# A group's maxima made into rows: one transposition and four masked copies in place of four transpositions and one copy

## The chip, the cores and the metric

The kernel runs on one core of a Trainium2 chip. The metric is the time of one execution on the device, in microseconds (us). The engines are named as the profile names them: PE is TensorE (matrix products), PEld its loads of stationary operands, DVE is VectorE, ACT is ScalarE, POOL is GpSimd, SP is the engine that issues most transfers. Each engine works through its own instructions in order and waits on semaphores for the others.

## The reference

A transformer block over x of shape (4, 512, 512): layer norm, attention over a context of 512 rows of width 256, residual, layer norm, and a feed-forward layer with ternary weights, residual. The attention has 32 heads of width 16:

```python
q = (x @ Wq).reshape(b, n, 32, 16)
k, v = jnp.split(ctx @ Wkv, 2, axis=-1)        # each to (b, 512, 32, 16)
q = apply_axial_rope(q, pos_map); k = apply_axial_rope(k, ctx_pos_map)
logits = jnp.einsum("bqhd,bkhd->bhqk", q, k) / 4
w = jax.nn.softmax(logits, axis=-1)
attn = jnp.einsum("bhqk,bkhd->bqhd", w, v).reshape(b, n, 512)
x = x + attn @ Wout + bout
...
h = gelu(bitlinear(layernorm(x), w_fc)); x = x + bitlinear(h, w_proj)
```

The change concerns the softmax alone: for each query and head the maximum over the keys is taken away from the logits before the exponential.

## The kernel before

**Groups and units.** The 32 heads of 4 batches are worked on in 32 groups `i` of four heads (`HG`), eight groups to a batch. A group has eight units `u`; each unit covers two heads. There are two passes over a group.

The first pass, `logits` (L423) and `maxima` (L437), has queries on the partitions: two products make a 128x1024 tile `lp` in PSUM (two heads, 512 keys each), and one DVE reduction takes the negated maximum along the keys, so that a group's eight units leave `mx`, 128 queries by 4 tiles of queries by 4 heads. At the last unit of the group `maxima` splits these 16 columns into a rounded high part (L441) and the rest (L442) and puts both into `mparts`, a tile of which two stand ready (groups take turns), filled with zeros once at the start (L168).

The second pass, `exponentials` (L462, L470, L474), has keys on the partitions: two products make `sp`, the transposed logits, and two more add the maxima to it. For these the maxima have to be rows: `mrows` has the queries along its free side (512 of them), and `sel` holds ones in the rows that belong to the wanted head. ACT then takes the exponential of the 128x1024 tile into `es`. `weigh` (L484) multiplies `es` with the values, eight products for every two units, into `av`.

**The maxima as rows.** `place_maxima` makes `mrows`. In `mparts` each of the four tiles of queries has a 128-column block of its own, in which 4 columns of each half are filled. Four transpositions on the PE (L449), one for each tile of queries, put the rows into one PSUM bank `mtp` of 128x512, and one ACT copy with a cast (L453) brings the bank to SBUF.

**What sets the order.** All five engines run in an order that the program writes out (`manual_schedule`). The units of the second pass (`s`) and those of the first pass (`l`, 13 to 15 units ahead) form one stream, cut in bursts of three. After each burst come the products of `weigh` that are due, and then at most one chore that finishes: a chore is a piece of other PE work with one PSUM bank `ps_t` of its own (a single buffer), such as the projections of queries, keys, values (`heads`, `values`: `qpq`, `kpk`, `vp`), the transpositions of normalised x (`tokens`: `xtp`) and the output projection (`projected`: `op`). What a chore leaves to other engines is put off to the next bursts (`put_off`): for `place_maxima`, the ACT copy at the head of the next burst. Chores are paid for with a credit that grows by 1.3 with each burst (1.1 late); `place_maxima` is urgent and goes in any case, but its cost, the last number of its `Chore`, is taken from the credit that other chores then lack. `lp` and `sp` share a pool of three PSUM tiles (`ps_s`), so a product into a fourth waits for the DVE reduction or the ACT exponential that reads the first.

**Elsewhere.** `make_sel` (L173) makes `sel` once before the first group. Rotations of queries and keys (`swap`, L353 to L359) run on DVE and POOL. The weights of the feed-forward layer are read in 32 chunks during the attention, summed (L569) and turned into signs by POOL (`low`, L585) and DVE (`ws`, L583). After the attention, from about 580 us, the feed-forward stage runs with almost nothing but L928 and L966 on the PE.

Of the kernel before, what the change touches and what calls it, by code (L numbers as in the profile page):

```python
# [9 lines left out]
F32 = mybir.dt.float32  # L10
F32R = mybir.dt.float32r
AF = mybir.ActivationFunctionType
ALU = mybir.AluOpType
AX = mybir.AxisListType

P = 128
# [15 lines left out]
def xattn_ffn(  # L32
# [13 lines left out]
    nc = tc.nc  # L46
# [3 lines left out]
    NT = S // P  # L50
# [17 lines left out]
    const = ctx.enter_context(tc.tile_pool(name="const", bufs=1))  # L68
# [25 lines left out]
    apool = attn.enter_context(tc.tile_pool(name="apool", bufs=2))  # L94
# [51 lines left out]
    ident = const.tile([P, P], F32, name="ident")  # L146
# [17 lines left out]

    mparts = []
    for i in range(2):
        mp = apool.tile([P, NT, P], F32, name=f"mparts{i}", tag=f"mparts{i}", bufs=1)
        nc.gpsimd.memset(mp, 0.0)  # L168
        mparts.append(mp)
    sel_col = const.tile([P, 2], F32, name="sel_col")  # L170
    sel = const.tile([P, 2, P], F32R, name="sel")

    def make_sel():  # L173
        nc.vector.tensor_reduce(
            sel_col,
            ident.rearrange("p (h c) -> p h c", h=2)[:, :, 0:4].rearrange(
                "p h (l r) -> p r h l", r=2
            ),
            AX.XY,
            ALU.add,  # L180
        )
        for r in range(2):
            nc.vector.tensor_scalar(sel[:, r, :], ones, sel_col[:, r : r + 1], None, ALU.mult)

# [54 lines left out]
    def put_off(k, f, end=0):  # L239
        later[end].setdefault(k, []).append(f)  # L240
# [174 lines left out]
    mx = {}  # L415
    mrows = {}
# [15 lines left out]
    def maxima(i, u, lp):  # L432

        t, r = divmod(u, 2)
        if u == 0:
            mx[i] = small.tile([P, NT, 2, 2], F32, name=f"mx{i}", tag="mx")
        nc.vector.tensor_reduce(mx[i][:, t, :, r], lp, AX.X, ALU.max, negate=True)  # L437
        if u == NU - 1:
            mp = mparts[i % 2].rearrange("p t (h c) -> p t h c", h=2)
            high = mp[:, :, :, 0:2]  # L440
            nc.vector.tensor_copy(high.bitcast(F32R), mx[i])  # L441
            nc.vector.tensor_tensor(  # L442
                mp[:, :, :, 2:4].bitcast(F32R), mx[i], high, ALU.subtract
            )

    def place_maxima(i):
        def step(tp, _):
            for t in range(NT):
                nc.tensor.transpose(tp[:, t * P : (t + 1) * P], mparts[i % 2][:, t, :], ident)  # L449

        def post(tp, k):
            mrows[i] = apool.tile([P, S], F32R, name=f"mrows{i}", tag="mrows")
            put_off(k + 1, lambda: nc.scalar.copy(mrows[i], tp))  # L453

        return Chore(f"mtp{i}", 1, step, post, 0.7)

    def exponentials(i, u):

# [248 lines left out]
    for what in "kq":  # L707
        chore(heads(0, 1, what))
    make_sel()
    load_x(1)  # L710
    nc.sync.dma_start(bout_sb, bout.to_broadcast([P, D]))
# [3 lines left out]
    for n in range(FIRST + 1):  # L715
        k0 += 1
        run(k0)
        if n < FIRST:
            lps[n] = logits(*divmod(n, NU))
        if n > 0:  # L720
            maxima(*divmod(n - 1, NU), lps.pop(n - 1))
        run(k0, 1)
        if fill:
            if fill[0].go():
                fill[0].post(fill[0].p, k0)
                fill.pop(0)
        if n == NU + 1:
            c = place_maxima(0)
            c.go()
            c.post(c.p, k0)  # L730
# [56 lines left out]
    for k, burst in enumerate(bursts):  # L787
        run(k)
        for kind, s in burst:
            i, u = divmod(s, NU)  # L790
            if kind == "l":
                lp = logits(i, u)
                maxima(i, u, lp)
                if u == NU - 1:
                    urgent.append((k + 1, place_maxima(i)))
                continue
# [16 lines left out]
            if u in (2, 6):  # L813
                c = 2 * i + u // 4
# [26 lines left out]
        while due and due[0][0] <= k:  # L841
            _, j, c, e = due.pop(0)
# [17 lines left out]
        while True:  # L860
            if open_chore is None:
# [5 lines left out]
                elif queue and queue[0].ready <= k and not used_bank and credit >= queue[0].cost:  # L867
                    c = queue[0]
# [51 lines left out]
    def xbank(name):  # L920
        return ps_x.tile([P, KD, P], F32, name=name, tag="x")
# [96 lines left out]
    with tc.manual_schedule(engines=ordered):  # L1018
# [15 lines left out]
        for n in range(len(steps) + 4):  # L1034
            on = n < len(steps)
            if on:
                b, f = steps[n]
# [5 lines left out]
            if on and b == 0 and 6 <= f < 6 + NT:  # L1043
                t = f - 6
                p = xbank(f"op{B - 1}_{t}").rearrange("p k n -> p (k n)")
# [8 lines left out]
                i = (B - 1) * NT + t  # L1054
                nc.vector.tensor_tensor(x_sb[:, i, :], p, x_sb[:, i, :], ALU.add)
            if on and b + 1 < B:
                at = (10, 11, 13, 14) if b == 0 else (6, 9, 12, 14)
                for t in range(NT):
                    i = (b + 1) * NT + t
# [95 lines left out]
```

## Time and profile before

| | us |
|---|---|
| median of 3 runs | 858.34 |
| lowest, highest | 857.26, 858.89 |
| the profiled execution, its own time | 856.57 |
| its span, first to last instruction | 854.8 |
| PE busy, DVE busy, ACT busy, POOL busy | 812.2, 619.7, 456.7, 287.1 |
| from 60 to 560 us (attention) | PE idle 11.1 of 500 |
| the four transpositions of L449, one group: their start to the next product | 0.58 to 0.59 |
| the copy of L453 | 0.587, 32 times |
| the exponential of L474 | 1.025, 256 times |
| the reduction of L437 | 1.216 mean, 256 times |

The profile is one execution, taken by the hardware. A busy share counts the time in which an instruction of that engine is under way; products on the PE overlap, so what a product really takes is read from the distance between starts, not from its own duration. An idle time is given with what ended it: the last of the things that the instruction waited for. The chain is the work that ended last, followed back from the end.

### The profile page before, as it was taken

The page shows a single profiled execution, that of the slowest core. Times are in us where ns is not written, and L with a number is a line of the kernel's source. Part 1 is how long each engine was busy: PE and PEld are TensorE (multiplying, and loading weights), DVE is VectorE, ACT ScalarE, POOL GpSimd, SP SyncE. Part 2 cuts the span into 40 slices and gives each one's busy share as a digit, 9 for nine tenths or more (in the row PEclk, how much of TensorE's full clock was granted, in tenths as well). Part 3 has the DMA queues.
Part 4 walks back from the last instruction along what each step waited for, and adds up shares of the span by engine and source line. Part 5 has one row for each costly group of instructions (what it writes and reads, how often), then busy time and mean ns, then how long its engine had stood idle before and what let it go on. Part 6 is the DMA issues. An engine that isn't in the chain of part 4 may idle for free.

```text
span 854.8 us, 13868 instructions
## 1 busy us (share of the span) xinstructions
PE 812.2 (95%) x5364; PEld 428.3 (50%) x5364; DVE 619.7 (72%) x852; ACT 456.7 (53%) x603; POOL 287.1 (34%) x287
## 2 busy tenths in 40 slices
PE   4699999999999899999999999998999999999996
PEld 1134433344333333433333334336668888888885
DVE  4789778788878988878678877825455864864755
ACT  2146766665665545666555665576234544554442
POOL 3017274653833564586515731301000100100000
PEclk9799999999999999999999999999999999999999
DMA  6875777567586576967645657432000100100101
GB/s 205 303 286 194 259 259 228 186 217 262 191 301 200 167 252 220 308 211 264 208 149 183 221 205 272 158 119 98 1 1 1 49 1 1 50 0 1 50 1 49
DMA packets 75561, 135.25 MB, mean 158 GB/s; under 512 B 10728, under 2 KB 12648, under 8 KB 74984
## 3 DMA queue, kind: packets, MB, share of 16 engines
q1 hardware_dynamic: 75088, 133.72, 45.8%
q8 instruction: 42, 0.69, 0.3%
q10 hardware_dynamic: 408, 0.66, 0.2%
q14 instruction: 23, 0.19, 0.1%
HBM read 79.30 MB, written 55.05 MB: 157 GB/s over the span
## 4 chain that ended last, share of the span: by engine, by line
PE 78%; DVE 12%; DMA 6%; issue 1%; ACT 1%; SPq 1%; POOL 1%; ACTq 0%; DVEq 0%; POOLq 0%
PE hp L928 14%; PE fp L966 14%; PE av L484 12%; PE sp L462 7%; PE lp L423 7%; DVE mx L437 7%; PE sp L470 5%; PE qpq L285 4%; PE op L285 4%; PE vp L285 3%; PE kpk L285 3%; PE op L1047 2%; PE mtp L449 1%; DVE ws L583 1%; DMA c_sb<-in_ctxT 1%
## 5 line engine op out<-in xcount | busy, mean ns | idle before, releaser
L437 DVE TENSOR_REDUCE mx<-lp 128x2 f32<-128x1024 f32 x256 | 305.3, 1216 | 86.0 <-PE lp L423 85.6
L474 ACT ACTIVATE es<-sp 128x1024 f32<-128x1024 f32 x256 | 254.5, 1025 | 146.6 <-PE sp L470 138.3
L484 PE MATMUL av<-es,va 128*32 128x512 f32 x1024 | 136.0, 604 | 0.0
L462 PE MATMUL sp<-q_st,k_st 64*128 64x512 f32 x512 | 115.1, 446 | 8.9 <-DVE mx L437 7.7
L423 PE MATMUL lp<-k_st,q_st 64*128 64x512 f32 x512 | 113.0, 437 | 9.4 <-DMA q_st<-q_d 7.4
L936 ACT ACTIVATE h<-hp,gam_fc 128x512 f32<-128x512 f32 x64 | 44.0, 688 | 129.1 <-PE hp L928 129.1
L966 PE MATMUL fp<-wproj,hh 128*128 128x512 f32 x256 | 103.5, 404 | 0.0
L928 PE MATMUL hp<-dTh,wfc 128*128 128x512 f32 x256 | 100.4, 392 | 1.2 <-ACT dTh L657 1.2
L470 PE MATMUL sp<-mrows,sel 64*128 64x512 f32 x512 | 101.2, 390 | 0.2 <-ACT mrows L453 0.2
L966 PE MATMUL fp<-wproj,hl 128*128 128x512 f32 x256 | 101.1, 395 | 0.0
L928 PE MATMUL hp<-dTl,wfc 128*128 128x512 f32 x256 | 100.4, 392 | 0.2 <-DVE dTl L658 0.2
L955 DVE TENSOR_TENSOR acc<-acc,h 128x512 f32<-128x512 f32 x56 | 38.7, 691 | 73.5 <-ACT h L936 73.5
L462 PEld LDWEIGHTS sp<-q_st,k_st 64*128 64x128 f32 x512 | 48.0, 184 | 83.1 <-DVE mx L437 42.6
L423 PEld LDWEIGHTS lp<-k_st,q_st 64*128 64x128 f32 x512 | 48.3, 185 | 80.8 <-ACT es L474 40.3
L523 POOL TENSOR_TENSOR aT<-aT,rb 128x512 f32<-128x512 f32 x16 | 21.1, 1320 | 133.3 <-DMA rb<-rden_d 112.1
L285 PE MATMUL qpq<-xT,wq_sb 128*32 128x512 f32 x512 | 62.3, 594 | 0.8 <-ACT xT L321 0.7
L928 PEld LDWEIGHTS hp<-dTh,wfc 128*128 128x128 f32 x256 | 48.2, 188 | 12.6 <-ACT dTh L657 2.1
L966 PEld LDWEIGHTS fp<-wproj,hl 128*128 128x128 f32 x256 | 48.3, 189 | 11.3 <-issue 0.7
L966 PEld LDWEIGHTS fp<-wproj,hh 128*128 128x128 f32 x256 | 48.2, 188 | 11.2 <-issue 0.7
L928 PEld LDWEIGHTS hp<-dTl,wfc 128*128 128x128 f32 x256 | 48.1, 188 | 11.0 <-DVE dTl L658 0.5
L470 PEld LDWEIGHTS sp<-mrows,sel 64*128 64x128 f32 x512 | 48.5, 185 | 5.9 <-ACT mrows L453 0.9
L196 POOL TENSOR_SCALAR r_a<-mv 128x1 f32<-128x1 f32 x16 | 4.7, 292 | 130.3 <-DVE mv L633 130.3
(129 smaller groups left out, 1036.0 us busy)
## 6 DMA issues: line engine op xcount, KB each, us to landing
k_st<-k_d SPq DMA_DIRECT2D x32, 512.0 KB
q_st<-q_d SPq DMA_DIRECT2D x32, 512.0 KB
k_d<-sh_k SPq DMA_DIRECT2D x32, 256.0 KB
k_d<-sl_k SPq DMA_DIRECT2D x32, 256.0 KB
q_d<-sh_q SPq DMA_DIRECT2D x32, 256.0 KB
q_d<-sl_q SPq DMA_DIRECT2D x32, 256.0 KB
av_d<-avs SPq DMA_DIRECT2D x32, 256.0 KB
wm<-in_wfcT SPq DMA_DIRECT2D x16, 256.0 KB
```

Source lines behind the costliest of these rows:

```text
L285: nc.tensor.matmul(p[j * HP : (j + 1) * HP, :], w[:, j * HP : (j + 1) * HP], x, start=start, stop=stop,)
L423: nc.tensor.matmul(lp[:, h, :], q_st[i][rows, r, t * P : (t + 1) * P], k_st[i][rows, r, :], start=True, stop=True,)
L437: nc.vector.tensor_reduce(mx[i][:, t, :, r], lp, AX.X, ALU.max, negate=True)
L462: nc.tensor.matmul(sp[:, h, :], k_st[i][rows, r, c * P : (c + 1) * P], q_st[i][rows, r, :], start=True, stop=False,)
L470: nc.tensor.matmul(sp[:, h, :], sel[rows, r, :], mrows[i][rows, :], start=False, stop=True)
L474: nc.scalar.activation(es, sp, AF.Exp, scale=1.0 / math.sqrt(HD))
L484: nc.tensor.matmul(av[j * HP : (j + 1) * HP, :], va[b % 2][:, c, v0 : v0 + HP], es[r][:, h, :], start=c == 0, stop=c == NT - 1,)
L523: nc.gpsimd.tensor_tensor(aT[b][:, n, :], aT[b][:, n, :], rb, ALU.mult)
L928: nc.tensor.matmul(hp, wfc_sb[k][:, f * P : (f + 1) * P], dT[b][half][:, k, :], start=half == 0 and k == 0, stop=half == 1 and k == KD - 1,)
L936: nc.scalar.activation(hid[b, f], hp, AF.Gelu, scale=gam_fc[:, 0:1])
L955: nc.vector.tensor_tensor(acc[b][0], old, x, ALU.add)
L966: nc.tensor.matmul(outs[b][t], parts[b, f][half][:, t * P : (t + 1) * P], wproj_sb[f], start=half == 0 and f == 0, stop=half == 1 and f == ...
```

## The change

`mparts` shrinks from four blocks to one of 128 columns: each half of 64 columns now holds 16 filled ones, ordered by head of the pair, high or low part, and tile of queries. One transposition gives a 128x128 block whose rows are the maxima of one head, part and tile. ACT then writes it four times, once for each tile of queries, into the four quarters of `mrows`, each time multiplied by a column of a mask that is one in the rows of that tile and zero in the others. `sel` picks all eight rows of a head, of which six hold zeros for any one query. `make_sel` makes the mask with one more reduction. The cost of the chore falls from 0.7 to 0.3.

```diff
-        mp = apool.tile([P, NT, P], F32, name=f"mparts{i}", tag=f"mparts{i}", bufs=1)
+        mp = apool.tile([P, P], F32, name=f"mparts{i}", tag=f"mparts{i}", bufs=1)
         nc.gpsimd.memset(mp, 0.0)
...
+    mask = const.tile([P, NT], F32, name="mask")
     def make_sel():
-        nc.vector.tensor_reduce(
-            sel_col,
-            ident.rearrange("p (h c) -> p h c", h=2)[:, :, 0:4].rearrange(
-                "p h (l r) -> p r h l", r=2
-            ),
-            AX.XY,
-            ALU.add,
-        )
+        rows = ident.rearrange("p (h c) -> p h c", h=2)[:, :, 0 : 4 * NT]
+        for dst, view in (
+            (sel_col, rows.rearrange("p h (r c) -> p r h c", r=2)),
+            (mask, rows.rearrange("p h (c t) -> p t h c", t=NT)),
+        ):
+            nc.vector.tensor_reduce(dst, view, AX.XY, ALU.add)
...
         if u == NU - 1:
-            mp = mparts[i % 2].rearrange("p t (h c) -> p t h c", h=2)
-            high = mp[:, :, :, 0:2]
+            mp = mparts[i % 2].rearrange("p (h c) -> p h c", h=2)[:, :, 0 : 4 * NT]
+            high, low = (
+                mp.rearrange("p h (r l t) -> p l t h r", r=2, l=2)[:, n] for n in range(2)
+            )
             nc.vector.tensor_copy(high.bitcast(F32R), mx[i])
-            nc.vector.tensor_tensor(
-                mp[:, :, :, 2:4].bitcast(F32R), mx[i], high, ALU.subtract
-            )
+            nc.vector.tensor_tensor(low.bitcast(F32R), mx[i], high, ALU.subtract)

     def place_maxima(i):
         def step(tp, _):
-            for t in range(NT):
-                nc.tensor.transpose(tp[:, t * P : (t + 1) * P], mparts[i % 2][:, t, :], ident)
+            nc.tensor.transpose(tp[:, 0:P], mparts[i % 2], ident)

         def post(tp, k):
             mrows[i] = apool.tile([P, S], F32R, name=f"mrows{i}", tag="mrows")
-            put_off(k + 1, lambda: nc.scalar.copy(mrows[i], tp))
-
-        return Chore(f"mtp{i}", 1, step, post, 0.7)
+
+            def spread():
+                for t in range(NT):
+                    nc.scalar.mul(
+                        mrows[i][:, t * P : (t + 1) * P], tp[:, 0:P], mask[:, t : t + 1]
+                    )
+
+            put_off(k + 1, spread)
+
+        return Chore(f"mtp{i}", 1, step, post, 0.3)
```

## The prediction

> **What bounds the kernel now.** First the page's busy times and chain, then the shares by stretch, then the single place of the change in the timeline.
>
> ```profile
> PE 812.2 (95%) x5364; PEld 428.3 (50%) x5364; DVE 619.7 (72%) x852; ACT 456.7 (53%) x603; POOL 287.1 (34%) x287
> ...
> PE 78%; DVE 12%; DMA 6%; issue 1%; ACT 1%; SPq 1%; POOL 1%; ACTq 0%; DVEq 0%; POOLq 0%
> ```
>
> The PE is busy for 95% and holds 78% of the chain. The Trainium skill (Perfetto Trace Analysis, "Identifying the Most-Contended Engine") warns that matmul busy time is a poor measure, because products overlap. So I looked at starts: in the attention the same two products follow each other at the same distance again and again (0.23 us for a pair of L462, L470 or L423), so the PE really has no gaps there. By stretch (PE, PEld, DVE, ACT, POOL busy):
>
> ```profile
> 60.00:160.00 100.00, 99.99 (x790) 40.64 (x788) 80.40 (x106) 62.95 (x76) 57.20 (x52) 1.00 0.66 219
> 260.00:360.00 100.00, 94.36 (x726) 37.87 (x728) 86.83 (x110) 56.50 (x66) 51.09 (x41) 1.00 0.66 221
> ```
>
> The PE leads, DVE is second with 80 to 87%, ACT has over a third free on average. In the second stretch DVE takes over in places. PE work that goes is therefore worth most of its time, but not all of it.
>
> The change sits here; the first fence is L449 and its reader, the second the timeline around one group (start, duration, instruction, idle before):
>
> ```profile
> L449 PE MATMUL mtp<-ident,mparts x128: 272/273/330, 50.1 to 561.3; 128*128 128x128 f32 x128
> L453 ACT CAST mrows<-mtp x32: 578/587/595, 50.8 to 562.9; 128x512 fp32r<-128x512 f32 x32
> ```
>
> ```profile
> 164.45 1.94 ACT L474 ACTIVATE es<-sp 128x1024 f32<-128x1024 f32 x2
> 164.97 0.66 PE L449 MATMUL mtp<-ident,mparts 128*128 128x128 f32 x4
> 165.56 0.49 PE L423 MATMUL lp<-k_st,q_st 64*128 64x512 f32 x2
> 165.90 0.50 PE L462 MATMUL sp<-q_st,k_st 64*128 64x512 f32 x2
> 166.24 0.39 PE L470 MATMUL sp<-mrows,sel 64*128 64x512 f32 x2
> 166.27 0.59 ACT L453 CAST mrows<-mtp 128x512 fp32r<-128x512 f32 x1
> 166.46 0.47 PE L423 MATMUL lp<-k_st,q_st 64*128 64x512 f32 x2
> ```
>
> The four transpositions take 0.59 us from their start to the next product. The first alone shows as 0.33 and all four as 0.66, so three more add 0.33: 0.11 us each, though each has a duration of 273 ns. The skill gives about 275 ns for a transposition inside a kernel (TensorE: Matmul & The Clock Gate, "Part 4: PE-mode transpose"); the duration agrees, but the price on a full PE is the 0.11.
>
> **The change part by part, for 32 groups.**
>
> *Three transpositions less.* 0.33 us a group, at most 32 x 0.33 = 10.6 us. What of it counts depends on what ends next, and the order written out gives only three places:
> - Between `weigh` and a product `lp` (9 groups: 95.3, 146.0, 195.4, 244.6, 299.7, 351.7, 403.5, 453.7, 499.7 us). ACT is idle before the copy and again before the next exponential. Whole gain: -3.0 us.
> - Between `weigh` and a product `sp` (12 groups). Four end in a wait for DVE (181.1, 281.5, 386.2, 487.6; the products after them wait up to 1.66 us for L437) and one leads into a stretch that DVE holds (533.2): nothing. Three (129.7, 229.9, 336.0) have a chore behind the burst: -1.0. The rest below, with ACT.
> - Right behind a product `sp` (11 groups), as in the fence. There ACT has two exponentials to work off; the second ends at 164.45 + 1.94 = 166.39, and the `lp` at 166.46 needs its bank. The PE arriving 0.33 earlier would wait for it. Eight of the eleven are pinned like this to within 0.1 us (-0.05 each), three have 0.3 to 0.5 of room (113.5, 319.8, 421.6): -0.4 - 0.9 = -1.3.
>
> *One ACT copy becomes four scaled ones.* Nothing in the trace is 128x128 from PSUM with a scale that is a column, so I bound it. Nearest row: the gelu L936, 128x512 from PSUM with such a scale, 688 ns; less 384 elements at 0.833 is 368 ns. The skill (ScalarE: Activation LUTs, "What ACT_TABLE_LOAD costs") has 186 ns plus 0.833 an element plus 93 for a column operand, 386 ns here, and an overlap of 93 ns back to back; the trace agrees on the overlap (two exponentials of 1.025 in 1.94, 0.11 less than their sum). So a start every 0.27 to 0.28, and four take 3 x 0.275 + 0.37 = 1.19 us against 0.587. Ends: without overlap 1.47; with the overhead hidden as in a copy followed by an exponential (starts 0.46 apart for 512 elements, so about 0.04 over the elements) 0.15 a piece, 0.8. I take 1.19: ACT is held 0.6 us longer, 20 us in all, hidden by its idle third except where an exponential behind it frees a bank for the PE. In the first place the exponential came 0.96 after the copy began and can now come at 1.10: 0.14 late, covered by the chore that follows. In the second it came at 0.72 and is now 0.38 late; where no chore follows (82.5, 439.2) the two `lp` behind it lose some 0.2 of the 0.33: -0.13 each, -0.3. In the third, it is late by 0.6, but ACT then idled 1.7 us. Two groups have the copy itself on the path: the first (50.1; L470 waited 0.25 for L453) +0.3, and the last (560.9, where exponentials are the chain) +0.6. The bank of `ps_t` comes free at the earliest 0.3 us before the next chore wants it: nothing, up to 0.2 a group if the four take 1.47.
>
> *DVE.* The two writes into `mparts` keep 16 elements and get one more stride; median 232 and 177 ns. Their maxima, 1282 and 1210, are stalls: the skill says that DVE and POOL share a port pair under an exclusive lock (SBUF — State Buffer, "SBUF: two separate sides"), and the long ones have a POOL instruction under way. (L441 for 1.28 us at 210.31, under the POOL's L356 from 210.28 to 211.56). I take no change, 0; at one end the longer pattern may cost 0.02 a group, at the other it may escape the lock, which would free up to (460 - 175) + (346 - 175) ns of DVE a group by the means, worth something only in the DVE stretches: -1 us at most. The mask costs one reduction of 128x32, by the 152 ns of L174 some 0.18 us, between L174 and L183; the first L437 began at 35.24, right behind, and 0.2 is made up while DVE next waits 1.34 for the PE: 0. If not, +0.2.
>
> *POOL.* Two memsets of 532 ns become about 204 each (as those of 128x128 at the start): nobody waits for them.
>
> *The credit.* Each group leaves 0.4 more: chores come up to six units earlier from unit 88 on (the transpositions for batch 3 at unit 130 instead of 136, `vp2_2` at 91 instead of 94), and with them their rotations on DVE and POOL, the transfers of `k_d`, `q_d` on SP and the loads of the next context. The last ones before the end stay, because they are tied to later units; between units 204 and 214 the PE is less full in both orders. PE work in total is the same, so 0; but POOL does its `low` (L585) in other company, and DVE waits in order for it (3.9 us in three waits now): +-2 us.
>
> **Sum:** -3.0 - 1.0 - 1.3 - 0.3 + 0.9 = -4.7 us; 856.57 becomes 851.9. The profiled execution lies 1.8 under the median of the runs, so against the median I forecast 858.34 - 4.7 = 853.6.
>
> **Rivals.**
> - *Everything counts* (the pinned places move along, as the exponentials are themselves fed by the PE): -10.6, 847.7. For it: 20 of the 32 transpositions are in the chain. Against: the bank waits above.
> - *A wash*: ACT takes back all that the PE gives, 858. PEld waits 40.3 us in 70 places for L474 already.
> - *Slower*: ACT decides. Place: the first and second exponential behind the four copies, whose banks the next `lp` products take. Price: the 0.63 of longer hold less the 0.33 saved, +0.3 a group, as soon as there is no slack between the end of an exponential and the product that reuses its bank; in half of the groups 16 x 0.3 = +4.8, 863. It decides if the four take over 1.3 us, or if earlier chores make ACT fuller where the copies fall. Against: chores follow the burst in most groups.
> - *The change doesn't do it* (more waits in the transposition): the instruction stream shows one L449 and four ACT writes a group, so no.
>
> **Numbers.** Forecast 0.46 (849 to 857), everything 0.14, wash 0.16, slower 0.24. A measurement here tells apart about 0.2%, 1.7 us. Faster: forecast, all of the first rival and a little of the wash, 0.62; same 0.15; slower 0.23. The range takes in the first rival and most of the last, 847.5 to 862.
>
> **What would show it.** L449 with 32 instructions and 0.25 us from its start to the next product; ACT on `mrows` 128 instructions of about 370 ns, four in 1.2 us; more idle time of PEld before `lp` ended by L474 than 40.3 us; L437 still about 1.2 us. I am wrong if four copies take far from 1.2 us, or if the stalls of DVE behind `low` or L449's neighbours grow by more than 3 us.

## The result and the profile after

| | before | changed kernel |
|---|---|---|
| median of 5 runs, us | 858.34 | 866.26 |
| lowest, highest | 857.26, 861.04 | 862.59, 867.39 |
| ratio, with its 95% interval | | 1.0079 [1.0051, 1.0107] |
| profiled execution: span, mean granted clock | 854.8, 0.993 | 864.5, 0.983 |
| feed-forward stage, in the trace | 273.4 | 273.4 |

The kernel became slower by 0.8%, where 0.55% faster was forecast. The feed-forward stage takes the same 273.4 us in both traces (from 581.39 to 854.8 and from 591.09 to 864.5), so the whole loss lies in the attention. Line numbers have moved: L449 is now L447, L453 is L454, L437 is L436, L441 and L442 are L442 and L443, L462, L470, L474 and L484 are L467, L475, L479 and L489, L423 is L422, L285 is L284, L585 is L590.

First the instructions that were exchanged, each tile's list of the changed kernel (count, then shortest, median and longest duration in ns):

```profile
L447 PE MATMUL mtp<-ident,mparts x32: 300/328/329, 50.8 to 570.0; 128*128 128x128 f32 x32
L454 ACT ACTIVATE mrows<-mtp,mask x128: 358/370/399, 51.1 to 572.8; 128x128 fp32r<-128x128 f32 x128
L442 DVE CAST mparts<-mx x32: 182/205/1279, 50.2 to 567.6; 128x16 fp32r<-128x16 f32 x32
L443 DVE TENSOR_TENSOR mparts<-mx,mparts x32: 187/192/1231, 50.5 to 567.8; 128x16 fp32r<-128x16 f32 x32
```

One transposition instead of four, four ACT writes of 370 ns, DVE writes that are hardly different. By these lines the change cost nothing. The page shows where time went; first two of its lines before the change, then those after:

```profile
L437 DVE TENSOR_REDUCE mx<-lp 128x2 f32<-128x1024 f32 x256 | 305.3, 1216 | 86.0 <-PE lp L423 85.6
L462 PEld LDWEIGHTS sp<-q_st,k_st 64*128 64x128 f32 x512 | 48.0, 184 | 83.1 <-DVE mx L437 42.6
```

```profile
PE 809.3 (94%) x5268; PEld 421.2 (49%) x5268; DVE 616.0 (71%) x853; ACT 472.1 (55%) x699; POOL 286.8 (33%) x287
...
PE   4699999999999899989999899898999999999996
...
PEclk9799999999999999999999899899999999999998
...
L436 DVE TENSOR_REDUCE mx<-lp 128x2 f32<-128x1024 f32 x256 | 305.8, 1216 | 99.7 <-PE lp L422 99.4
...
L467 PEld LDWEIGHTS sp<-q_st,k_st 64*128 64x128 f32 x512 | 48.4, 186 | 90.1 <-DVE mx L436 54.0
```

The PE lost 96 instructions and is busy 2.9 us less, in a span that is 9.7 us longer: it stands still more. No reduction is slower (1216 ns in both), but DVE waits 99.4 us for `lp` (85.6 before), the PE's loads wait 54.0 us for the reduction (42.6 before), and POOL's `low` waits 50.6 us for DVE (40.9 before). PE and DVE wait for each other more, in turn. The loads' wait for the exponential, which would have shown ACT as the cause, went only from 40.3 to 42.7. Near the end of the attention two slices (475 to 497 and 540 to 562 us) have an 8 both in the row of the PE and in that of its clock.

**Where.** The start of a run up to the first transposition scatters between 50.1 and 54.4 us from trace to trace, and what follows the last transposition is 293.9 to 294.5 in nearly all. So I measure from the transposition of group 0 to that of group 31, 510.80 us before. The changed kernel takes 8.44 more. At group 14 it is still 1.22 ahead, at group 25 it is level, at group 27 it is 5.29 behind, at group 30 5.38, at group 31 8.44. Stretches of both traces (from:to and length; busy us and instructions of PE, PEld, DVE, ACT, POOL; granted clock, share of the transfers, GB/s), groups 25 to 27 before and after:

```profile
472.69:499.73 27.04, 26.19 (x197) 10.60 (x195) 23.61 (x28) 18.54 (x22) 20.44 (x18) 1.00 0.60 217
```

```profile
473.36:505.72 32.36, 28.71 (x190) 10.97 (x188) 25.24 (x26) 19.37 (x27) 17.49 (x15) 0.89 0.64 225
```

The same stretch of work has 3.65 us of idle PE in place of 0.85, and a clock of 0.89; the PE is busy 2.5 us longer with seven instructions less.

**What differs there** is the pace of the chores. Before, the last projection of queries goes one step of eight products to a burst, four times; the timeline of the PE before the change (start, duration, instruction):

```profile
475.53 1.04 PE L285 MATMUL qpq<-xT,wq_sb 128*32 128x512 f32 x8
...
479.13 1.04 PE L285 MATMUL qpq<-xT,wq_sb 128*32 128x512 f32 x8
...
482.12 1.04 PE L285 MATMUL qpq<-xT,wq_sb 128*32 128x512 f32 x8
...
484.45 1.06 PE L285 MATMUL qpq<-xT,wq_sb 128*32 128x512 f32 x8
```

After, three of the four steps go at once and the fourth in the next burst, and the bursts that follow have no chore, or only the transposition of the maxima (the brackets give the idle time before an instruction and what ended it):

```profile
477.60 2.75 PE L284 MATMUL qpq<-xT,wq_sb 128*32 128x512 f32 x24
...
482.52 1.04 PE L284 MATMUL qpq<-xT,wq_sb 128*32 128x512 f32 x8
...
487.51 0.49 PE L422 MATMUL lp<-k_st,q_st 64*128 64x512 f32 x2 [0.33 <-ACT es L479]
488.85 0.50 PE L467 MATMUL sp<-q_st,k_st 64*128 64x512 f32 x2 [0.84 <-DVE mx L436]
...
491.29 0.33 PE L447 MATMUL mtp<-ident,mparts 128*128 128x128 f32 x1 [0.48 <-DVE mparts L443]
492.63 0.50 PE L467 MATMUL sp<-q_st,k_st 64*128 64x512 f32 x2 [1.01 <-DVE mx L436]
```

What DVE does meanwhile: its two writes into `mparts` for this group in the timeline before, then after with the POOL operations beside them:

```profile
485.36 0.26 DVE L441 CAST mparts<-mx 128x16 fp32r<-128x16 f32 x1
...
485.65 0.63 DVE L442 TENSOR_TENSOR mparts<-mx,mparts 128x16 fp32r<-128x16 f32 x1
```

```profile
488.67 1.28 POOL L353 TENSOR_TENSOR oth_q<-oth_q,trig 128x512 f32<-128x512 f32 x1
488.83 1.16 DVE L442 CAST mparts<-mx 128x16 fp32r<-128x16 f32 x1
...
489.91 1.28 POOL L354 TENSOR_TENSOR rot_q<-rot_q,trig 128x512 f32<-128x512 f32 x1
490.03 1.21 DVE L443 TENSOR_TENSOR mparts<-mx,mparts 128x16 fp32r<-128x16 f32 x1
```

The two writes of 16 elements, 182 and 187 ns at best, take 1.16 and 1.21 us, each ending within 0.05 us of the POOL operation beside it (489.95 and 491.19). Those POOL operations belong to the queries' rotation, which the early projection brought here. In the two groups these writes take 2.74 us in place of 1.33, and `ws` 3.30 in place of 2.71. The sum of such stalls doesn't decide: over the whole trace the writes take 26.4 us, against 25.8 before and 29.6 in the fastest kernel of the experiments (e5). What is argued here is that their place does.

Worked out from the starts in the timeline of before: a unit of the second pass takes the PE 0.56 (483.10 to 483.66), one of the first pass 0.23 and a `weigh` 0.99, so a group without chores takes 8 x 0.56 + 8 x 0.23 + 4 x 0.99 = 10.3 us, 1.9 for each of its 5.3 bursts, and a step of a chore adds 1.0. DVE is busy for 23.61 / 2 = 11.8 us a group in the stretch above, 2.2 a burst. By this estimate, which spreads DVE's work evenly, a burst with a step is bound by the PE and a bare one, without a chore, by DVE: a step taken out of a burst and put into another that has one already does not cancel out.

### The profile page after: what moved, and what is told of

It reads as the page before. It is cut to its first block, busy times and chain, and to the rows that moved or that the text cites. A ratio compares the mean times of both kernels' runs of the same rounds, so it can differ in the third digit from the quotient of the medians.

```text
span 864.5 us, 13767 instructions
## 1 busy us (share of the span) xinstructions
PE 809.3 (94%) x5268; PEld 421.2 (49%) x5268; DVE 616.0 (71%) x853; ACT 472.1 (55%) x699; POOL 286.8 (33%) x287
## 5 line engine op out<-in xcount | busy, mean ns | idle before, releaser
L436 DVE TENSOR_REDUCE mx<-lp 128x2 f32<-128x1024 f32 x256 | 305.8, 1216 | 99.7 <-PE lp L422 99.4
L479 ACT ACTIVATE es<-sp 128x1024 f32<-128x1024 f32 x256 | 255.1, 1027 | 148.6 <-PE sp L475 138.0
L489 PE MATMUL av<-es,va 128*32 128x512 f32 x1024 | 139.0, 617 | 0.0
L467 PE MATMUL sp<-q_st,k_st 64*128 64x512 f32 x512 | 116.5, 451 | 13.9 <-DVE mx L436 11.4
L422 PE MATMUL lp<-k_st,q_st 64*128 64x512 f32 x512 | 114.1, 441 | 15.6 <-DMA q_st<-q_d 8.2
L475 PE MATMUL sp<-mrows,sel 64*128 64x512 f32 x512 | 102.3, 395 | 1.3 <-ACT mrows L454 1.3
L467 PEld LDWEIGHTS sp<-q_st,k_st 64*128 64x128 f32 x512 | 48.4, 186 | 90.1 <-DVE mx L436 54.0
L422 PEld LDWEIGHTS lp<-k_st,q_st 64*128 64x128 f32 x512 | 49.0, 187 | 87.6 <-ACT es L479 42.7
L284 PE MATMUL qpq<-xT,wq_sb 128*32 128x512 f32 x512 | 61.3, 594 | 0.8 <-ACT xT L320 0.7
L933 PEld LDWEIGHTS hp<-dTh,wfc 128*128 128x128 f32 x256 | 48.2, 188 | 12.7 <-ACT dTh L662 2.1
L475 PEld LDWEIGHTS sp<-mrows,sel 64*128 64x128 f32 x512 | 49.0, 188 | 7.2 <-ACT mrows L454 2.0
```

The source lines that it names most:

```text
L284: nc.tensor.matmul(p[j * HP : (j + 1) * HP, :], w[:, j * HP : (j + 1) * HP], x, start=start, stop=stop,)
L422: nc.tensor.matmul(lp[:, h, :], q_st[i][rows, r, t * P : (t + 1) * P], k_st[i][rows, r, :], start=True, stop=True,)
L467: nc.tensor.matmul(sp[:, h, :], k_st[i][rows, r, c * P : (c + 1) * P], q_st[i][rows, r, :], start=True, stop=False,)
L475: nc.tensor.matmul(sp[:, h, :], sel[rows, r, :], mrows[i][rows, :], start=False, stop=True)
L479: nc.scalar.activation(es, sp, AF.Exp, scale=1.0 / math.sqrt(HD))
L489: nc.tensor.matmul(av[j * HP : (j + 1) * HP, :], va[b % 2][:, c, v0 : v0 + HP], es[r][:, h, :], start=c == 0, stop=c == NT - 1,)
```

## The experiments

Theories at the start: the loss comes from the credit, that is from 0.7 becoming 0.3, by which chores are taken up earlier; or from the four ACT writes; or from the new layout of `mparts` and its transposition. Letters in the expectations stand for theories as described there; C holds that chores taken three steps at a time do the harm, F that the number of bare bursts in a stretch decides, H that the work which a chore leaves to DVE and POOL collides. Each kernel has 5 to 22 runs; ratios are to the kernel before measured beside it. The last column is the distance from group 0 to group 31 less the 510.80 of before, in one trace each.

| kernel | median, us | ratio, 95% interval | distance |
|---|---|---|---|
| the change | 866.26 | 1.0079 [1.0051, 1.0107] | +8.44 |
| changed, cost 0.7 (e1) | 854.63 | 0.9963 [0.9952, 0.9975] | -4.25 |
| before, cost 0.3 (e2) | 865.66 | 1.0095 [1.0077, 1.0113] | +6.88 |
| before, four ACT writes (e3) | 858.23 | 1.0008 [0.9996, 1.002] | -1.94 |
| changed, cost 0.7, one ACT write (e4) | 854.01 | 0.9963 [0.995, 0.9976] | -3.55 |
| changed, slower credit (e5) | 852.95 | 0.9933 [0.991, 0.9955] | -4.71 |
| before, faster credit (e6) | 866.4 | 1.0094 [1.0064, 1.0124] | +8.45 |
| changed, two steps a burst (e7) | 870.42 | 1.014 [1.0114, 1.0165] | +8.96 |
| e1, two steps a burst (e8) | 854.88 | 0.9959 [0.9944, 0.9975] | -1.13 |
| early in the middle only (e9) | 859.8 | 1.0014 [0.999, 1.0038] | -0.94 |
| early in the tail only (e10) | 866.09 | 1.0085 [1.0059, 1.011] | +6.85 |
| changed, still slower credit (e11) | 863.0 | 1.0044 [1.002, 1.0069] | +3.62 |
| e10, work behind the chores later (e12) | 862.41 | 1.0037 [1.0015, 1.0058] | +2.91 |
| e9, work behind the chores later (e13) | 863.66 | 1.0057 [1.0038, 1.0077] | +5.89 |

**e1: the change without its cost.** The changed kernel with

```diff
-        return Chore(f"mtp{i}", 1, step, post, 0.3)
+        return Chore(f"mtp{i}", 1, step, post, 0.7)
```

> The changed kernel (one transposition, four masked copies), with the chore's cost put back to 0.7, so that all chores stand where they stood before the change. Theory A (the credit: chores moved forward leave the PE bare from about unit 198 to 213 and from unit 231, where DVE then sets the pace and the granted clock falls): the two losses of 5.3 us between 473 and 506 us and 3 us between 554 and 570 us go, granted clock back at 0.99, 853 to 857 us, a little under the kernel before. Theory B (four copies hold ACT 0.55 us longer a group and the PE waits for the exponentials behind them): stays near 864 to 866.

Faster by 0.37%, 3.2 us. Its chores stand in the order of the kernel before. In the stretch from group 25 to 27 nothing of the loss is left:

```profile
473.19:500.22 27.03, 25.88 (x190) 9.99 (x188) 23.58 (x28) 19.47 (x28) 20.99 (x18) 1.00 0.64 227
```

**e2: the cost without the change.** The kernel before with

```diff
-        return Chore(f"mtp{i}", 1, step, post, 0.7)
+        return Chore(f"mtp{i}", 1, step, post, 0.3)
```

> The kernel before (four transpositions, one copy), with the chore's cost at 0.3: only the chores move, as they do in the change. Theory A: slower than before, 863 to 868 us, with the granted clock under 0.99 in the same stretches. Theory B: within 2 us of before, 857 to 860.

Slower by 0.95%. One number in the planner makes the whole loss, with four transpositions and one copy as before. The same stretch:

```profile
479.38:509.50 30.12, 26.74 (x197) 10.71 (x195) 25.13 (x26) 18.24 (x21) 17.54 (x15) 1.00 0.70 243
```

It is 3.1 us longer than before at a full clock, with 3.38 us of idle PE: the loss is there without any fall of the clock. DVE is busy 1.5 us longer with two instructions less: some of them are stretched (the writes of `mparts` take 2.70 us in place of 1.33, `ws` 3.33 in place of 2.71).

**e3 and e4: the four ACT writes alone, and the transposition alone.** e3 is the kernel before with four writes of a quarter each in place of one copy; e4 is e1 with one ACT write that spreads the block to all four quarters, so the mask is left out.

```diff
 # e3
-            put_off(k + 1, lambda: nc.scalar.copy(mrows[i], tp))
+            def spread():
+                for t in range(NT):
+                    nc.scalar.mul(mrows[i][:, t*P:(t+1)*P], tp[:, t*P:(t+1)*P], ones[:, t:t+1])
+            put_off(k + 1, spread)
 # e4
-                for t in range(NT):
-                    nc.scalar.mul(mrows[i][:, t*P:(t+1)*P], tp[:, 0:P], mask[:, t:t+1])
+                nc.scalar.copy(mrows[i].rearrange("p (t q) -> p t q", t=NT),
+                               tp[:, 0:P].unsqueeze(1).to_broadcast([P, NT, P]))
```

> The kernel before with its one copy on ACT split into four of 128x128 with a column of ones as the scale; four transpositions and the cost of 0.7 stay. It prices the copies alone. Theory A: four copies take 1.14 us against 0.587, mostly hidden: 858 to 862 us. Theory B: 32 groups lose 0.3 to 0.55 each, 867 to 875.

> One transposition and one ACT copy, which reads the 128 columns four times over into the 512 of the rows; the mask is left out, so each query gets the maxima of all four tiles; cost 0.7. It prices the three transpositions less, with ACT as before. If the PE's 0.33 us a group counts in most groups: 849 to 853 us. If the pinned places swallow it: 855 to 858.

Four writes in place of one change nothing that can be measured (1.0008, and its interval holds 1), though ACT is busy for 15.6 us more (472.3 against 456.7). e4, without them, is as fast as e1 with them. So ACT is cleared, and the gain belongs to the rest of the change: one transposition in place of four, with the layout that goes with it.

**e5 and e6: the pace of the credit.** The cost is not needed for the loss if it is the pace that matters. e5 is the change, cost 0.3, with less credit for each burst; e6 the kernel before, cost 0.7, with more.

```diff
 # e5
-    RATE, RATE_END = 1.3, 1.1
+    RATE, RATE_END = 1.225, 1.025
 # e6
-    RATE, RATE_END = 1.3, 1.1
+    RATE, RATE_END = 1.375, 1.175
```

> The changed kernel with the cost of 0.3, and the credit's growth cut from 1.3 and 1.1 to 1.225 and 1.025 a burst, by the 0.4 that a group leaves over its 5.3 bursts. Chores stand within a unit of where they stood before the change (on average 0.03 units later), three steps in one burst occur 7 times (before 6, changed 11). If the pace of the credit is the cause: like the changed kernel with the cost of 0.7, 852 to 857 us. If the low cost hurts in another way: 860 to 866.

> The kernel before with its cost of 0.7, and the credit's growth raised to 1.375 and 1.175. Chores come 2.5 units earlier on average from unit 88 on, as in the change, three steps in one burst 10 times. If the pace of the credit is the cause: 862 to 868 us. If not: 857 to 860.

A group has 8 units of each pass, 16 units, a little over five bursts; 0.4 less cost to a group is 0.075 a burst, and that is what the rates give back or take. e5 puts every chore within a unit of its place before, and is the fastest kernel of all: 0.67% under before, though its interval touches those of e1 and e4. e6 loses as much as e2. The cost of 0.3 does no harm by itself; the earlier chores do.

**e7 and e8: at most two steps a burst.** In the changed kernel 11 bursts take three steps of chores, before the change 6. e7 limits the changed kernel to two, e8 the kernel of e1.

```diff
+        taken = 0
         while True:
...
-            if not must and credit < open_chore.cost:
+            if not must and (credit < open_chore.cost or taken == 2):
                 break
             credit -= open_chore.cost
+            taken += open_chore.steps > 1
```

> The changed kernel with the cost of 0.3, in which a burst takes at most two steps of chores (bar those that an urgent chore forces). Chores come 2.4 units early on average, as in the change, but three steps in one burst fall from 11 to 2. Theory C (clumps: three steps, 2.75 us of chore on the PE, leave DVE and ACT without work, and the bursts after it stand bare and go at DVE's pace): most of the loss goes, 853 to 858 us. Theory D (chores that come early run out early, whatever their size, and their work on DVE, POOL and SP falls in with the weights'): stays at 862 to 867.

> The changed kernel with the cost of 0.7 and at most two steps of chores a burst: chores where they stood before, three steps in one burst 3 times in place of 6. Theory C: a little faster than with the cost of 0.7 alone (854.6), 852 to 855 us. Theory D: the same as that.

Theory C falls: with smaller lumps, chores as early as before the limit (2.4 units ahead of the kernel before, on average from unit 88), the time is the worst of all; with cost 0.7 the limit does nothing. Where e7 loses, the clock has a part. Between groups 14 and 21 it takes 129.22 us where the change takes 123.77, and all of the difference is PE busy time (120.83 against 115.36 us) at a mean clock of 0.95 against 1.00; the change has its falls of the clock later. Over the runs the mean clock is 0.976 to 0.984 in e7 and 0.982 to 0.992 in the change. Why the median is 4 us higher isn't shown beyond that.

**e9 and e10: early only in the middle, or only in the tail.** Groups' costs are chosen so that chores run ahead in one part and are back in step in the other.

```diff
 # e9
-        return Chore(f"mtp{i}", 1, step, post, 0.3)
+        return Chore(f"mtp{i}", 1, step, post, 0.3 if i < 21 else 1.5 if i < 24 else 0.7)
 # e10
-        return Chore(f"mtp{i}", 1, step, post, 0.3)
+        return Chore(f"mtp{i}", 1, step, post, 0.7 if i < 23 else -0.8)
```

> The changed kernel with the cost of 0.3 for groups 0 to 20, 1.5 for 21 to 23 and 0.7 from then on: chores come early exactly as in the change up to unit 172 and stand where they stood before from unit 190 on. Theory F (it is the bare tail, units 184 to 213, in which the changed order has three bursts more without a chore): 854 to 857 us, nearly the whole loss gone. Theory G (the loss lies in the middle, where the work behind the early chores meets that of the weights and the PE's clock drops): 858 to 863.

> The changed kernel with the cost of 0.7 for groups 0 to 22 and -0.8 from then on: chores stand as before up to unit 180 and come early from unit 183 on, with three bursts more without a chore from 184 to 213 as in the change (and two more behind 214). Theory F: 859 to 865 us. Theory G: 854 to 857.

Both cost: e9 0.5% against e1 (1.0014 / 0.9963), e10 1.2% (1.0085 / 0.9963). Their sum is more than the 1.16% between the change and e1, because e10 goes further than the change: one more lump of three steps and two more bare bursts behind unit 214, where it loses 3.9 us against e1 from group 27 to 30, the change 0.5. In the trace of the change against that of e1 (12.7 us in all), 3.8 lie before group 25, 5.3 between 25 and 27 and 3.1 between 30 and 31: some two thirds in the tail.

**e11: fewer bare bursts.** Between units 198 and 213 the kernel before has four bursts without a chore, and so have e1 and e5; the change has six. With less credit still, one is left.

```diff
-    RATE, RATE_END = 1.3, 1.1
+    RATE, RATE_END = 1.18, 1.0
```

> The changed kernel with the cost of 0.3 and the credit's growth at 1.18 and 1.0: chores come later than before, ten steps of them in units 198 to 213 in place of four, and one bare burst there in place of four (six in the change). Theory F: faster than with 1.225 and 1.025 (852.95), 849 to 852 us. Theory G: 853 or more.

Theory F falls in this form: with one bare burst in place of four the kernel takes 863.0 us, where 849 to 852 was expected. From group 25 to 27 it takes 33.15 us, but with six steps of chores more than e1 there (239 instructions of the PE against 190), which is 6 us of work at 1.0 a step. Its loss lies in the groups before: it had these steps still to do at group 25 and yet was 1.8 us behind e1. Chores that come late (some four units behind on average) are no better than early ones.

**e12 and e13: the work behind the chores.** What a projection leaves for DVE and POOL (`swap`, with its casts) and its stores to memory are put off by two bursts more, for the projections of the tail in e12 and of the middle in e13.

```diff
 # e12, on e10
-            put_off(k + 1, swap, 1)
+            late = 2 * ((b, n) in ((3, 2), (3, 3)))
+            put_off(k + 1 + late, swap, 1)
...
-            d = 1 if prologue[0] else 4
+            d = (1 if prologue[0] else 4) + late
 # e13, on e9: the same, with
+            late = 2 * ((b, n) in ((2, 2), (2, 3), (3, 0), (3, 1)))
```

> The kernel with an early tail alone (866.09), in which what the last four projections of queries and keys leave to DVE, POOL and SP (shuffle, rotation, stores) starts two bursts later, so that it stands within a burst of where it stood before the change while the products on the PE stay early. Theory H (the work behind the chores: POOL's rotations come between the weights' signs, DVE waits in order for them and for the port, the PE for DVE): 856 to 860 us. Theory I (the PE: early chores in lumps, then bursts without any, in which DVE sets the pace and the clock falls): stays at 863 to 868.

> The kernel with an early middle alone (859.8), in which the work behind the eight projections of queries and keys from unit 106 to 153 starts two bursts later, about where it stood before. Theory H: 854 to 857 us. Theory I: 858 to 862.

In the tail this gives back part of the loss: 862.41 us in place of 866.09, between what theory H expected (856 to 860) and theory I, by which the loss is the PE's own lumps and bare bursts (863 to 868). Groups 25 to 27 of e10 and of e12:

```profile
472.58:503.55 30.97, 27.31 (x190) 10.62 (x188) 25.20 (x26) 19.24 (x27) 17.50 (x15) 0.94 0.66 237
```

```profile
472.20:500.61 28.41, 26.06 (x190) 10.08 (x189) 24.09 (x28) 19.36 (x27) 21.80 (x18) 1.00 0.65 224
```

2.6 of the 3.9 us over e1's 27.03 are gone, DVE is busy 1.1 us less with two instructions more, and the clock is full again: half of the 2.6 is idle time of the PE, half its busy time (27.31 against 26.06). What differs is POOL's order: in e10 a rotation of keys stands ahead of a `low`, for which DVE waits, and one of queries ahead of an attention output (`aT`), in e12 and before the change behind them. The stores moved along, so POOL and the transfers aren't told apart. In the middle the same delay made it worse: e13 takes 131.37 us from group 14 to 21 against 123.85 of e9. Most of that is the clock: of the 7.5 us 6.5 are PE busy time (121.50 against 114.98) at a mean clock of 0.94 against 1.00; by the medians the delay costs 3.9 us. So theory H agrees with two thirds of what e10 loses between groups 25 and 27; for the middle it is refuted, as 854 to 857 us was expected there. The rest of e10's loss, behind group 27, is unchanged in e12.

## Why the prediction was wrong

**What held.** The sum for the instructions was -4.7 us. Without the earlier chores it measures -3.2 us (-2.1 to -4.1 by the interval of e1) and, in the trace, -4.25; e5 has -4.71 in the trace and 0.67%, 5.7 us, by its ratio. Of its parts:
- *Transpositions.* 32 of them, 0.26 us from start to the next product (473.36 to 473.62), against 0.25 forecast: 0.33 saved a group. That less than half of 10.6 us counts is what e1 shows. The places held less well. From each transposition to the next, e1 against before gains 1.8 us in the nine groups of the first kind (3.0 forecast), 1.3 in the three with a chore behind the burst (1.0), 0.1 in the eight pinned ones (0.4), nothing in the three that were to have room (0.9), 0.65 in the five that were counted for nothing, and 0.5 in the two where ACT was to take a part back (0.3). So the sum is near the measured gain in part by luck.
- *ACT.* 370 ns against 368, four in 1.14 us against 1.19, so one starts every 0.257 us, 0.11 before its predecessor ends. (The 0.63 of longer hold in the slower rival should be 0.60 by the prediction's own figures; it is 0.55.) Hidden, as forecast: e3 and e4. Only at the end it shows: from the last transposition to the end e1 takes 294.42 us where before takes 293.89, +0.5 against +0.6 forecast, and e4, with one write, 293.88. The first group's +0.3 is not to be seen at the next transposition. The loads' wait for the exponential rose by 2.4 us, as foretold in direction. So the slower rival, ACT deciding at +4.8 and 863 us, comes near the time and is the wrong mechanism: had it been right, e3 would have been slower and e1 not faster.
- *DVE and POOL operations.* Medians 205 and 192 in place of 232 and 177: nothing, as forecast. Memsets 212 against 204.
- *The wash and the full gain* fall with e1.

**The step that failed** is the credit: "PE work in total is the same, so 0; but POOL does its `low` (L585) in other company [...]: +-2 us." It costs 0.95% alone (e2), 8.2 us, and 1.0079 / 0.9963, 1.16% or 10 us, in the changed kernel. What was listed was right: chores up to six units earlier, with their rotations and transfers, and a PE that is less full between units 204 and 214. That the price of the earlier chores was wrong is shown by e1, e2, e5 and e6. What makes them cost is shown only in part; three things were left out.

First, "the same PE work in total" gives 0 only if the PE is the bound in every burst. It is not: the loads' waits for the reduction above are such places, and by the estimate above bursts without a chore go at DVE's pace. The kernel before had four of them between units 198 and 213, the change six; a step that leaves a burst where DVE is close behind saves less there than it costs where it goes. This is argued from the two traces, and e11 shows that the number of bare bursts alone doesn't decide. The prediction's own lines had DVE at 87% and PE at 94% from 260 to 360 us.

Second, the effect on DVE was looked for only in `low`, in three waits of 3.9 us. Between groups 25 and 27 DVE was hit elsewhere: in the writes of `mparts` beside POOL's operations and the reductions that stand behind them, as shown at 488 to 491 us, and the transposition and the next product wait for those. Putting the work behind the tail's chores off by two bursts won back 2.6 of 3.9 us there (e12).

Third, a PE that waits is not only idle; in three places the change got a lower clock afterwards, where the trace of before has none in the attention. This is told below.

The prediction's own test, "I am wrong if [...] the stalls of DVE behind `low` or L449's neighbours grow by more than 3 us", looked near the right place but not at it: DVE waits 4.2 us for `low` against 3.9. What grew by more than 3 us is the wait of the PE's loads (L467, before L462) for the reduction, by 11.4. The range of +-2 us for this step was an opinion and had no row behind it; the place to find one was the stretch with the bare bursts.

**What stays open.** Why early chores cost some 4 us in the middle (e9) is not settled: the delay of their work made it worse, and no single wait stands out. The clock has a part: the five runs of e9 with a mean clock of 0.989 or more took 855.83 to 860.26 us, the four with 0.985 or less 860.56 to 864.54; but at an equal 0.987 e9 took 858.5 to 862.9 and e1 855.58 to 857.21, so some 2.6 us remain. Why late chores cost (e11) isn't settled either. What the runs do show: of the orders tried with the changed instructions, those within a unit of the order before (e1, e5) or close to it (e8) are the fastest, and the others (the change, e7, e9 to e13) cost between 0.5% and 1.8% against e1, whether chores come early or late.

## What to carry to other kernels

A number in a planner is a change of schedule: when an operation gets cheaper and its cost in the planner follows, run the two edits apart, and, if the order was good, give the freed credit back in the rate (e5 kept the gain that the change lost). "The total work of the busiest engine is unchanged" prices a move at nothing only if that engine is the bound both where the work leaves and where it arrives; compare PE and DVE burst by burst, not over the span. And follow a moved piece to the other engines: here the work that it brought along for POOL, DVE and the stores made up part of the loss in the tail.

## What the runs showed of the hardware that I had not expected

**The clock can halve after a window of 3.41 us in which the PE is half idle.** Stretches of the changed kernel, the columns as above:

```profile
471.10:474.50 3.40, 1.65 (x11) 0.67 (x9) 3.40 (x6) 1.99 (x3) 3.17 (x4) 0.93 1.05 289
474.50:477.40 2.90, 2.90 (x14) 1.18 (x18) 2.90 (x3) 2.12 (x6) 2.90 (x3) 0.50 1.06 396
...
552.60:556.00 3.40, 2.03 (x11) 0.92 (x11) 3.33 (x7) 2.51 (x6) 1.34 (x4) 0.99 0.03 5
556.00:562.60 6.60, 6.36 (x30) 2.17 (x28) 3.83 (x4) 3.34 (x5) 3.89 (x4) 0.50 0.22 50
...
281.60:285.00 3.40, 1.20 (x10) 0.48 (x6) 3.40 (x5) 1.79 (x5) 0.33 (x1) 1.00 0.43 129
```

After stretches of 3.4 us in which the PE was busy for 1.65 and 2.03 the granted clock falls to 0.50; the falls last 3.4 and 6.8 us (474.05 to 477.46 and 555.97 to 562.79; the third of the attention goes from 494.52 to 497.94). At 281.6 us it was busy for only 1.20 of 3.4 and the clock stayed full; the kernel before has 1.57 there, also at full clock. The Trainium skill (TensorE: Matmul & The Clock Gate, "Part 1: The HAM clock gate") says that the gate looks at windows of some 3.4 us that run freely, and halves the clock after one idle window. The traces agree on the windows: in each of the fifteen the changes of the clock lie whole multiples of 3.41 us apart, and where these windows begin differs from trace to trace. They don't agree that a window has to be idle: the longest gap before the first fall was 1.42 us, before the one at 556 us 0.94.

Counted in these windows, from 60 to 580 us of all fifteen traces and where the clock was full, the rows fall into place. After all 9 windows with the PE busy for less than 1.75 us the clock halved; with 1.75 to 2.1 it did so after 12 of 25, with 2.1 to 2.5 after 2 of 50, and with more than 2.5 after none of 2163. The three windows before the falls of the change have 2.00, 2.06 and 2.00 us. The 1.20 us at 281.6 is split by a border: the two windows there (279.49 to 282.90 and 282.90 to 286.32) have 2.47 and 2.17. So in these runs a window that is half idle can be enough, and whether a spell of waiting fills one is chance. The cost is seen in equal work of the changed kernel, eight products of L489:

```profile
557.12 1.93 PE L489 MATMUL av<-es,va 128*32 128x512 f32 x8
...
564.19 1.06 PE L489 MATMUL av<-es,va 128*32 128x512 f32 x8
```

Of the five runs of the change, the three with a mean clock of 0.982 to 0.986 took 866.26 to 867.39 us and the two with 0.991 and 0.992 took 863.47 and 862.59: some 4 us go with the falls of the clock, and the two runs with the higher clock are still slower than the median before.
